# A gated recurrence of 512 steps: the first groups' input products put in front of half A's and half B's first products

## The chip, the cores and the metric

The kernel runs on one core of one Trainium2 chip. The metric is the device time of one execution in microseconds (us), the median over several runs. A lower number is better.

## The reference

A recurrence over 512 time steps for 8 sequences, with 512 input values and 512 state values each; its output is added to the input.

```python
def step(h, x_t):
    fused = sigmoid(concat([x_t, h]) @ w_W + w_b)
    hidden_state, output_state = split(fused, 2)          # r and z below
    memory_state = x_t @ wx_W + wx_b + hidden_state * (h @ wh_W + wh_b)
    h_new = output_state * h + (1.0 - output_state) * tanh(memory_state)
    return (h_new, h_new)

out = x + scan(step, cond, x)      # x: (8, 512, 512), cond: (8, 512), all float32
```

Each step needs three products with the state h (for r, z and the memory term) and three with the input x_t. Only those with h hang on the step before.

## The kernel before, in words

**Halves and banks.** The 512 state values are split into half A and half B. The state of each half is in the tiles `hTA` and `hTB`, one for each of eight steps in turn. The products with the state go to three PSUM banks: A (192 columns: memory term, z and r of half A; weights `wa`), B (128 columns: r and the memory term of half B) and C (64 columns: z of half B; in the tile `cs`). The weights of B and C are in `wb`. A product such as A0 or B2 names the bank and the quarter k of the state that it multiplies; k = 0 and 1 are in `hTA`, 2 and 3 in `hTB`. Each is four matmuls (`mm`, line 217) on four column tiles of TensorE, and the trace has two records for a matmul. The function `mm` issues all matmuls, so all have line 217 and are told apart by their tiles.

**Order in a step.** TensorE takes the products of a step in the order `ORDER`, and then some work on the inputs of later steps. The first step has an order of its own, `FIRST`, in which `x` stands for one part of input products. The schedule is manual: every engine does its instructions in the order in which the program lists them, and the framework adds the waits.

**Gates.** For each half, VectorE transposes r, the memory term and z out of PSUM (`turn_r`, `turn_h`, `turn_z`; lines 407 and 423), ScalarE takes the sigmoids, VectorE scans r times the memory term (`memory`), ScalarE takes the tanh, and a second scan (`update`, both line 391) makes the new state, on which the next step's products wait. Half B's gates come behind half A's on VectorE, and `update` of half A behind half B's `turn_r` and `turn_h`. GpSimd adds x (line 545) and SyncE stores.

**Input products.** Four steps make a group. Group g's products with `wx` are accumulated in `xps[g % 2]` (tiles `xp`), a PSUM tile with 384 columns of products (`XC`) that is first filled with the bias: `seed(g)`, a ScalarE copy. Groups 0 to 3 are plain products: `prefill(g)` is a generator of four parts (k = 0 to 3), each four matmuls of 384 columns, and `take(it, n)` issues n parts. From group 4 on the products of two groups are made together from seven products of sums (`x_step`, `product`), which need sums of weights: `weight_sum(n)` on VectorE, into the tiles `tw`, and sums of inputs on GpSimd. A finished group is copied by ScalarE to `even` or `odd`, from there into the banks A, B and C of the group's steps (`spread`), and VectorE transposes its memory term out of it (`turn_x`, line 280). Group 0 is read straight from `xps[0]`, and in the first step the A products are accumulated in `xps[0]` itself (`to`, `pa`).

**The start.** `warm()` is a product with zeros. SyncE's queue brings `wx` in four parts, `wa` in four parts, `wb` in two and the second half of chunk 0's inputs (`load_x(0, 1)`, which holds groups 2 and 3), in this order; the first half comes with the initial state in `head`, by ScalarE's queue. Chunks 1 to 3 follow in the first steps. Group 1's parts stand between the A products of the first step and behind it; groups 2 and 3 stand behind steps 1 to 4, two parts a step.

```python
        if i < 5:
            take(first[(i + 3) // 2], 2)
        if i > 3:
            x_step(*divmod(i, 2 * GS))
```

Of the kernel before, what the change touches and what calls it, by code (L numbers as in the profile page):

```python
# [24 lines left out]

ORDER = "A0 B0 A1 A2 A3 B1 B2 B3 C0 C1 C2 C3"

FIRST = "A0 x A1 x A2 x A3 B0 B1 B2 B3 C0 C1 C2 C3"

BANKS = {"A": 192, "B": 128, "C": 64}  # L30

# [3 lines left out]
XC = slice(64, 448)  # L35
# [14 lines left out]
XP = {"A": slice(0, 192), "X": slice(192, 320), "C": slice(320, 384), "B": slice(384, 512)}  # L50
# [3 lines left out]
def tile_cond_rnn_residual(  # L54
# [39 lines left out]
    nc = tc.nc  # L94
# [30 lines left out]
    def load_x(c, half=slice(0, 2)):  # L125

        if c < NCH:
            if c not in xins:
                xins[c] = xin_p.tile([P, 2, NQ, TC * B // 2], F32, tag="xin", name=f"xin_{c}")
            nc.sync.dma_start(  # L130
                out=xins[c][:, half], in_=x[c].rearrange("p (e k n) -> p e k n", e=2, k=NQ)[:, half]
            )

    def x_of(c, k, t, n):

        e, t = divmod(t, TC // 2)
        if c == 0 and e == 0:
            first = head[:, :NX].rearrange("p (k n) -> p k n", k=NQ)
            return first[:, k, t * B : (t + n) * B]
        return xins[c][:, e, k, t * B : (t + n) * B]  # L140
# [10 lines left out]
    wa = const.tile([P, NQ, NQ, 192], F32, name="wa")  # L151
    for k in range(NQ):
        nc.sync.dma_start(out=wa[:, k], in_=wa_d[k])
    wb = const.tile([P, NQ, NQ, 192], F32, name="wb")
    nc.sync.dma_start(out=wb[:, :3], in_=wb_d)
    nc.sync.dma_start(out=wb[:, 3], in_=wb3_d)

    def wh(bank, k, j):
        return wa[:, k, j] if bank == "A" else wb[:, k, j, {"C": slice(0, 64), "B": slice(64, 192)}[bank]]

    load_x(0, 1)

    def pair(n, name, rows, slots):

# [32 lines left out]
    even = const.tile([P, 512], F32, name="even")  # L197
    odd = const.tile([P, 512], F32, name="odd")

    def state(hf, i, slot=2):  # L200

        s = i % GS
        return hT[hf][i % NH][:, B * s : B * s + B, :, slot]
# [9 lines left out]
    xps = [psum.tile([P, 512], F32, name=f"xp{q}") for q in range(2)]  # L213
    eps = psum.tile([P, 512], F32, name="eps")[HI, :W]

    def mm(out_, lhsT, rhs, start=False):
        nc.tensor.matmul(  # L217
            out_, lhsT, rhs, start=start, stop=False, skip_group_check=True
        )
# [4 lines left out]
    def warm():  # L224

        mm(xps[1], zeros[:, :128], zeros)
# [18 lines left out]
    def act(key, out_, in_, func, **kw):  # L245
        inst = nc.scalar.activation(out_, in_, func, **kw).ins  # L246
        if key in written:
            tc.declare_no_dep(inst, written[key], reason="ordered through VectorE")
        written[key] = inst
        return inst  # L250

    def seed(g):

        nc.scalar.copy(xps[g % 2], bias)  # L254

    def prefill(g):

        c, t0 = divmod(g * GS, TC)
        for k in range(NQ):
            for j in range(NQ):  # L260
                mm(
                    xps[g % 2][32 * j : 32 * j + 32, XC],
                    x_of(c, k, t0, GS),
                    wx[:, k, j, :],
                )
            yield

    def source(g):

        return xps[0] if g == 0 else (even, odd)[g % 2]  # L270

    def spread(g, names):

        for n in names:
            nc.scalar.copy(banks[g % 2][n], source(g)[:, XP[n]])

    def turn_x(g, hf):

        c0 = XP["X"].start + HU * hf
        nc.vector.transpose(  # L280
            md1[hf][g % 2][:, :, :, 1].rearrange("p n c -> p c n"), source(g)[:, c0 : c0 + HU]
        )
# [4 lines left out]
    def wx_of(kh, ch):  # L287
        return wx[:, 2 * kh : 2 * kh + 2, 2 * ch : 2 * ch + 2]
# [5 lines left out]
    def weight_sum(n, k=slice(0, 2), j=slice(0, 2)):  # L294

        a, b = [
            (wx_of(0, 1), wx_of(0, 0)),
            (wx_of(1, 1), tw[0]),
            (wx_of(1, 1), wx_of(0, 1)),
            (wx_of(1, 0), tw[1]),  # L300
        ][n]
        nc.vector.tensor_tensor(tw[n][:, k, j], a[:, k, j], b[:, k, j], ALU.subtract)
# [44 lines left out]
    def take(it, n=None):  # L347
        while n is None or n > 0:
            if next(it, it) is it:
                return  # L350
            n = None if n is None else n - 1

    seed(1)
    take(prefill(0))
    warm()
    first = {g: prefill(g) for g in (1, 2, 3)}
    weight_sum(2)
    weight_sum(0)
    spread(0, "BCA")
    for hf in range(2):  # L360
        turn_x(0, hf)

    pool_done = {}
    for i in range(T):
        g, s = divmod(i, GS)
        c, t = divmod(i, TC)
        ps = banks[g % 2]
# [4 lines left out]

        for n in (ORDER if i else FIRST).split():
            if n == "x":
                take(first[1], 1)
                continue
            bank, k = n[0], int(n[1])
            hs = hT[k // 2][i % NH][:, :, k % 2, 2]
            for j in range(NQ):
                to = ps[bank] if i or bank != "A" else xps[0][:, XP["A"]]  # L380
                mm(to[32 * j : 32 * j + 32, :], hs, wh(bank, k, j))
        if i < 5:
            take(first[(i + 3) // 2], 2)
        if i > 3:
            x_step(*divmod(i, 2 * GS))

# [2 lines left out]
        def scan(c_, out_, d0, d1):  # L389

            return nc.vector.tensor_tensor_scan(  # L391
                *[t_[:, :, c_].rearrange("p n c s -> p (n c s)") for t_ in (out_, d0, d1)],
                0.0,
                ALU.mult,
                ALU.add,
            ).ins

        pa = ps["A"] if i else xps[0][:, XP["A"]]
        raw = {
            "h": (pa[:, :HU], ps["B"][:, HU:]),  # L400
            "z": (pa[:, HU : 2 * HU], ps["C"]),
# [3 lines left out]
        def turned(n, hf):  # L405
            t_ = work.tile([P, 2, 32], F32, tag=f"t{n}{hf}", name=f"t{n}{hf}_{i}")
            inst = nc.vector.transpose(t_.rearrange("p c n -> p (c n)"), raw[n][hf]).ins  # L407
            return t_[:, :, rows], inst
# [4 lines left out]
        def turn_r(hf):  # L413
            tr, _ = turned("r", hf)
            r_done[hf] = act(
                ("r", hf, g % 2, s),
                md0[hf][g % 2][:, rows, :, 1].rearrange("p n c -> p c n"),
                tr,
                AF.Sigmoid,
            )  # L420
# [27 lines left out]
        def memory(hf, q):  # L448

            c_ = slice(q, q + 1)  # L450
            scan(c_, ms[hf], md0[hf][g % 2][:, rows], md1[hf][g % 2][:, rows])
            act(("n", hf, q, i % NH), state(hf, i, 1)[:, :, c_], ms[hf][:, :, c_, 1], AF.Tanh)
# [8 lines left out]
        turn_z(0)  # L461
        memory(0, 0)
        memory(0, 1)
        turn_r(1)
        turn_h(1)
        update(0, 0)
        turn_z(1)
        tc.add_manual_dep(update(0, 1), r_done[1].name, SYNC)
        if i == 0:

            seed(2)
        if i == T - 1:
            nc.gpsimd.tensor_tensor(
                ot[:, t, :2, :].rearrange("p c n -> p n c"),
# [13 lines left out]
        o, u = divmod(i, 2 * GS)  # L488
        nxt, two = o + 1 < NG // 2, o + 2 < NG // 2
        if i == 0:  # L490
            nc.scalar.copy(odd[:, XC], xps[1][:, XC])
        if u == 0:
            spread(2 * o + 1, "AC")
            turn_x(2 * o + 1, 0)
            turn_x(2 * o + 1, 1)
        elif u == 1:
            if o and nxt:
                nc.vector.tensor_tensor(reg(GA), reg(BE), more[HI], ALU.add)
                nc.scalar.copy(even[LO, XC], reg(AL))
            spread(2 * o + 1, "B")  # L500
        elif u == 2:
            if o == 0:
                nc.scalar.copy(even[:, XC], xps[0][:, XC])
                seed(3)
            elif nxt:
                nc.vector.tensor_tensor(odd[HI, XC], reg(GA), both[LO], ALU.add)
                nc.scalar.copy(both[HI], reg(DE))
            if two:
                x_sum(o + 2, 2)
        elif u == 3:  # L510
            if two:
                nc.scalar.copy(reg(AL), bias[LO, XC])
                x_sum(o + 2, 0)
        elif u == 4:
            if o == 0:
                nc.scalar.copy(odd[:, XC], xps[1][:, XC])
            elif nxt:
                nc.vector.tensor_tensor(even[HI, XC], reg(BE), both[HI], ALU.add)
            if two:
                nc.scalar.copy(reg(DE), step_bias[HI])  # L520
        elif u == 5 and nxt:
            if o:
                nc.scalar.copy(odd[LO, XC], reg(GA))
            spread(2 * o + 2, "A")
            turn_x(2 * o + 2, 0)
        elif u == 6 and nxt:
            spread(2 * o + 2, "BC")
            turn_x(2 * o + 2, 1)
            if two:
                nc.scalar.copy(more[HI], eps)  # L530
                x_sum(o + 2, 1)
        elif u == 7 and nxt:
            if two:
                nc.scalar.copy(reg(BE), reg(AL))
                nc.scalar.copy(both[LO], reg(DE))
                x_sum(o + 2, 3)
# [105 lines left out]
```

## Time and profile before

| | us |
|---|---|
| median of 3 runs (lowest, highest) | 1657.39 (1656.86, 1657.92) |
| the profiled execution: its own time | 1659.38 |
| its span in the trace | 1657.4 |
| TensorE matmuls busy | 1645.1 (99% of the span) |
| TensorE weight loads busy (beside the matmuls) | 1487.9 (90%) |
| ScalarE busy | 1198.4 (72%) |
| VectorE busy | 1152.0 (70%) |
| GpSimd busy | 303.2 (18%) |

The engines are PE (TensorE matmuls), PEld (TensorE weight loads), DVE (VectorE), ACT (ScalarE), POOL (GpSimd) and SP (SyncE, which issues DMAs). Rows of a timeline give start and duration in us, the engine, the line of the kernel, the operation, output<-input with the program's tile names, shapes and the count of records merged; in brackets stands the idle time before it and what ended it. Rows of windows give the stretch, its length, the busy time and count of PE, PEld, DVE, ACT and POOL, the granted TensorE clock as a share of full speed, the DMA share and GB/s. Times of several records merged count from the first start to the last end, so a pipelined group's duration is longer than the time by which it holds up the next.

### The profile page before, as it was taken

To read this page: it belongs to the slowest core of one execution; us is meant where nothing else is said; L and a number is where in the kernel's file an instruction comes from. 1 tells how busy PE (TensorE), PEld (TensorE's weight loads), DVE (VectorE), ACT (ScalarE), POOL (GpSimd) and SP (SyncE) were. 2 spreads that over 40 slices of the span, in tenths; PEclk is the share of its full clock that TensorE was granted. 3 is DMA by queue.
4 is the path that set the end of the run, shared out by engine and by line. 5 is a ranking of instruction groups with operands and counts; after the bars stand their busy time and mean duration, and the time that the engine had idled before them with its cause. 6 is when DMAs were issued, how large, how long until landed. Compare 5 with 4: busy or idle time off the path is not lost.

```text
span 1657.4 us, 126070 instructions
## 1 busy us (share of the span) xinstructions
PE 1645.1 (99%) x54253; PEld 1487.9 (90%) x54253; DVE 1152.0 (70%) x9193; ACT 1198.4 (72%) x6009; POOL 303.2 (18%) x1283
## 2 busy tenths in 40 slices
PE   8999999999999999999999999999999999999998
PEld 5999999999888889999999999999999999989987
DVE  5776676676766766767667667676676676766766
ACT  4777777777777777777777777777777777777775
POOL 1211111111111111111111111111111111111111
PEclk9999999999999999999999999999999999999999
DMA  4000000000000000000000000000000000000000
GB/s 182 11 14 17 15 14 15 17 15 14 14 16 16 14 14 16 16 14 14 16 16 14 15 16 16 15 14 16 16 15 14 16 16 15 14 16 11 10 10 10
DMA packets 37287, 31.16 MB, mean 19 GB/s; under 512 B 4084, under 2 KB 35060, under 8 KB 36600
## 3 DMA queue, kind: packets, MB, share of 16 engines
q1 hardware_dynamic: 36576, 22.95, 4.5%
q8 instruction: 424, 6.95, 1.7%
q14 instruction: 135, 1.11, 0.2%
q10 hardware_dynamic: 152, 0.16, 0.0%
HBM read 14.70 MB, written 8.39 MB: 14 GB/s over the span
## 4 chain that ended last, share of the span: by engine, by line
PE 98%; DVE 1%; DMA 1%; issue 0%; ACT 0%; SPq 0%
PE A L217 40%; PE B L217 26%; PE xp L217 17%; PE cs L217 13%; PE eps L217 1%; DMA wx<-in_wx_dram 1%; DVE tr L407 0%; DVE m L391 0%; DVE tz L407 0%; DVE md1B L423 0%; DVE hTA L391 0%; DVE md1A L423 0%; SPq L149 0%; ACT hTB L246 0%; ACT xp L254 0%
## 5 line engine op out<-in xcount | busy, mean ns | idle before, releaser
L217 PE MATMUL A<-wa,hTA 128*32 128x192 f32 x8176 | 547.6, 326 | 2.1 <-DVE hTA L391 2.1
L217 PE MATMUL A<-wa,hTB 128*32 128x192 f32 x8176 | 440.7, 326 | 0.0
L217 PE MATMUL B<-wb,hTA 128*32 128x128 f32 x8192 | 440.6, 273 | 0.0
L217 PEld LDWEIGHTS A<-wa,hTA 128*32 128x32 f32 x8176 | 281.3, 122 | 129.8 <-DVE hTA L391 103.7
L407 DVE STREAM_TRANSPOSE tr<-A 128x64 f32<-128x64 f32 x511 | 127.6, 250 | 369.4 <-PE A L217 369.4
L545 POOL TENSOR_TENSOR ot<-xin,hTB 128x16 f32<-128x16 f32 x503 | 125.9, 250 | 1309.3 <-DVE hTB L391 989.0
L217 PEld LDWEIGHTS B<-wb,hTA 128*32 128x32 f32 x8192 | 337.5, 122 | 5.7
L217 PEld LDWEIGHTS A<-wa,hTB 128*32 128x32 f32 x8176 | 323.0, 122 | 13.0 <-DVE hTB L391 0.4
L217 PE MATMUL B<-wb,hTB 128*32 128x128 f32 x8192 | 332.2, 273 | 0.0
L217 PE MATMUL xp<-tw,sx 128*32 128x96 f32 x1488 | 267.5, 433 | 0.0
L217 PEld LDWEIGHTS B<-wb,hTB 128*32 128x32 f32 x8192 | 255.1, 122 | 0.0
L246 ACT ACTIVATE md0A<-tr 128x16 f32<-128x16 f32 x512 | 112.3, 219 | 191.3 <-DVE tr L407 177.4
L391 DVE TENSOR_TENSOR_SCAN hTB<-hd0B,hTB 128x24 f32<-128x24 f32 x1024 | 157.8, 195 | 100.5 <-ACT hTB L246 100.5
L217 PE MATMUL cs<-wb,hTA 128*32 128x64 f32 x8192 | 222.9, 219 | 0.0
L217 PE MATMUL cs<-wb,hTB 128*32 128x64 f32 x8192 | 222.8, 219 | 0.0
L217 PE MATMUL xp<-wx,xin 128*32 128x384 f32 (+2 forms) x1304 | 219.6, 425 | 0.0
L217 PEld LDWEIGHTS cs<-wb,hTA 128*32 128x32 f32 x8192 | 200.4, 122 | 0.0
L391 DVE TENSOR_TENSOR_SCAN hTA<-hd0A,hTA 128x24 f32<-128x24 f32 x1024 | 190.1, 186 | 0.0
L246 ACT ACTIVATE hd0B<-tz 128x16 f32<-128x16 f32 x512 | 116.0, 227 | 93.3 <-DVE tz L407 93.3
L246 ACT ACTIVATE hTB<-hTB 128x16 f32<-128x16 f32 x512 | 120.1, 234 | 78.9 <-DVE hTB L391 53.1
L217 PEld LDWEIGHTS cs<-wb,hTB 128*32 128x32 f32 x8192 | 173.0, 122 | 0.0
L246 ACT ACTIVATE hTA<-m 128x8 f32<-128x8 f32 x1024 | 160.6, 206 | 2.8 <-DVE m L391 0.5
(105 smaller groups left out, 2664.3 us busy)
## 6 DMA issues: line engine op xcount, KB each, us to landing
out_dram<-ot SPq DMA_DIRECT2D x128, 64.0 KB, 1.6
xin<-in_x_dram SPq DMA_DIRECT2D x112, 64.0 KB, 2.2
wx<-in_wx_dram SPq DMA_DIRECT2D x4, 768.0 KB, 6.9
wa<-in_wa_dram SPq DMA_DIRECT2D x4, 384.0 KB, 8.9
wb<-in_wb_dram SPq DMA_DIRECT2D x1, 1152.0 KB
xin<-in_x_dram SPq DMA_DIRECT2D x3, 256.0 KB, 8.3
wb<-in_wb_dram SPq DMA_DIRECT2D x1, 384.0 KB, 11.2
head<-in_xh_dram ACTq DMA_DIRECT2D x1, 144.0 KB, 4.9
```

The source lines that it names most:

```text
L217: nc.tensor.matmul(out_, lhsT, rhs, start=start, stop=False, skip_group_check=True)
L246: inst = nc.scalar.activation(out_, in_, func, **kw).ins
L391: return nc.vector.tensor_tensor_scan(*[t_[:, :, c_].rearrange("p n c s -> p (n c s)") for t_ in (out_, d0, d1)], 0.0, ALU.mult, ALU.add,).ins
L407: inst = nc.vector.transpose(t_.rearrange("p c n -> p (c n)"), raw[n][hf]).ins
L545: return engine.tensor_tensor(ot[:, t, 2 * hf : 2 * hf + 2, :].rearrange("p c n -> p n c"), x_of(c, slice(2 * hf, 2 * hf + 2), t, 1).rearr ...
```

## The change

Group 1's four parts are issued whole behind group 0's, before the first step, and `warm()` is dropped. The first step's order becomes all of A, then group 2's four parts, then B and C. Group 3's parts come one a step behind steps 1 to 4, and the first step has no part behind C. The first step's A products go to bank A, like those of all steps. The second half of chunk 0 is loaded before `wb`. On VectorE the first weight sum follows the two `turn_x` and the second stands in the first step between the halves' gates. On ScalarE `seed(2)`, the copy of group 1 to `odd` and `seed(3)` come before the first step; group 2's copy to `even` takes the place that group 1's copy had behind the first step. From step 5 on every engine has the same instructions in the same order as before.

```diff
-FIRST = "A0 x A1 x A2 x A3 B0 B1 B2 B3 C0 C1 C2 C3"
+FIRST = "A0 A1 A2 A3 x x x x B0 B1 B2 B3 C0 C1 C2 C3"
...
         nc.sync.dma_start(out=wa[:, k], in_=wa_d[k])
+    load_x(0, 1)
     wb = const.tile([P, NQ, NQ, 192], F32, name="wb")
     nc.sync.dma_start(out=wb[:, :3], in_=wb_d)
     nc.sync.dma_start(out=wb[:, 3], in_=wb3_d)
...
-    load_x(0, 1)
...
     seed(1)
     take(prefill(0))
-    warm()
-    first = {g: prefill(g) for g in (1, 2, 3)}
-    weight_sum(2)
-    weight_sum(0)
-    spread(0, "BCA")
+    take(prefill(1))
+    first = {g: prefill(g) for g in (2, 3)}
+    spread(0, "ABC")
     for hf in range(2):
         turn_x(0, hf)
+    weight_sum(2)
+    seed(2)
+    nc.scalar.copy(odd[:, XC], xps[1][:, XC])
+    seed(3)
...
             if n == "x":
-                take(first[1], 1)
+                take(first[2], 1)
                 continue
...
-                to = ps[bank] if i or bank != "A" else xps[0][:, XP["A"]]
-                mm(to[32 * j : 32 * j + 32, :], hs, wh(bank, k, j))
-        if i < 5:
-            take(first[(i + 3) // 2], 2)
+                mm(ps[bank][32 * j : 32 * j + 32, :], hs, wh(bank, k, j))
+        if 1 <= i < 5:
+            take(first[3], 1)
...
-        pa = ps["A"] if i else xps[0][:, XP["A"]]
+        pa = ps["A"]
...
         memory(0, 1)
+        if i == 0:
+            weight_sum(0)
         turn_r(1)
...
-        if i == 0:
-
-            seed(2)
...
         if i == 0:
-            nc.scalar.copy(odd[:, XC], xps[1][:, XC])
+            nc.scalar.copy(even[:, XC], xps[0][:, XC])
...
         elif u == 2:
-            if o == 0:
-                nc.scalar.copy(even[:, XC], xps[0][:, XC])
-                seed(3)
-            elif nxt:
+            if o and nxt:
```

## The prediction

> **What bounds the kernel now.** I read the profile's page first, then the chain of waits in order of time, then the timeline of the first 40 us, then the windows with the granted clock, and last the DMA issues.
>
> ```profile
> span 1657.4 us, 126070 instructions
> PE 98%; DVE 1%; DMA 1%; issue 0%; ACT 0%; SPq 0%
> ```
>
> The chain that ended last is TensorE (PE) for 98% of the span, so outside the first microseconds the time is the sum of PE's instructions. One step in order of time, first steps, then a later one:
>
> ```profile
> 23.07 0.88 PE A L217 x16
> 23.94 0.65 PE B L217 x24
> ...
> 30.25 0.33 PE A L217 x8
> 30.57 0.22 PE B L217 x8
> 30.79 0.97 PE A L217 x24
> 31.76 0.65 PE B L217 x24
> 32.42 0.45 PE cs L217 x32
> 32.87 1.29 PE xp L217 x16
> 34.16 0.33 PE A L217 x8
> ...
> 44.60 0.33 PE A L217 x8
> ...
> 47.22 0.65 PE xp L217 x7
> 47.87 0.33 PE A L217 x8
> ```
>
> Columns: start, duration, engine, tile, records (a matmul leaves two). The step that starts at 30.25 lasts 3.91 us without a hole: 2.62 for A, B and C (cs), then 1.29 for two parts of plain x products. The step at 44.60 carries 0.65 of x work and lasts 3.27. So a part of plain x products (4 matmuls, 8 records) is 0.65 us, a whole group of four parts 2.58, the A products of a step 1.31 (0.33 + 0.97), B 0.87, C 0.45, and a step is as long as PE's work in it.
>
> PE is not full only at the start. The timeline there:
>
> ```profile
> 11.15 0.85 PE L217 MATMUL xp<-wx,head 128*32 128x384 f32 x8 [0.48 <-DMA wx<-in_wx_dram]
> 11.23 3.43 DVE L302 TENSOR_TENSOR tw<-wx 128x1536 f32<-128x1536 f32 x2 [2.01 <-DMA wx<-in_wx_dram]
> 12.34 0.33 ACT L275 COPY A<-xp 128x192 f32<-128x192 f32 x1
> 14.74 0.21 DVE L280 STREAM_TRANSPOSE md1B<-xp 128x64 f32<-128x64 f32 x1
> 15.05 0.86 PE L217 MATMUL xp<-wa,hTA 128*32 128x192 f32 x8 [1.99 <-issue]
> 19.99 0.64 PE L217 MATMUL B<-wb,hTA 128*32 128x128 f32 x16
> 20.25 0.25 DVE L407 STREAM_TRANSPOSE tr<-xp 128x64 f32<-128x64 f32 x1 [5.30 <-PE xp L217]
> 21.12 0.25 DVE L407 STREAM_TRANSPOSE tr<-B 128x64 f32<-128x64 f32 x1
> 21.64 0.14 PEld L217 LDWEIGHTS A<-wa,hTA 128*32 128x32 f32 x4 [0.19 <-DVE hTA L391]
> 21.98 0.59 ACT L254 COPY xp<-bias 128x512 f32<-128x512 f32 x1
> 22.81 0.31 DVE L391 TENSOR_TENSOR_SCAN hTB<-hd0B,hTB 128x24 f32<-128x24 f32 x2 [0.73 <-ACT hTB L246]
> 23.07 0.51 PEld L217 LDWEIGHTS A<-wa,hTB 128*32 128x32 f32 x16 [0.41 <-DVE hTB L391]
> ...
> 23.28 0.46 ACT L491 COPY odd<-xp 128x384 f32<-128x384 f32 x1
> ...
> 24.81 0.23 DVE L407 STREAM_TRANSPOSE tr<-B 128x64 f32<-128x64 f32 x1
> 25.89 0.31 DVE L391 TENSOR_TENSOR_SCAN hTB<-hd0B,hTB 128x24 f32<-128x24 f32 x2 [0.20 <-ACT hTB L246]
> ```
>
> Three losses show. First, group 0's products end about 11.8 (11.15 + 0.65). A0 starts only at 15.05, just after VectorE's transposes out of xp end at 14.95 (14.74 + 0.21): the two weight sums, 3.43 us, stand ahead of them. Second, from 15.05 to 19.99 PE does A's 32 records and three parts of x, which at the prices above are 1.31 + 1.94 = 3.25, in 4.94: 1.69 lost. The windows say why; the third column from the right is the granted clock:
>
> ```profile
> 13.00:15.00 2.00, 0.06 (x1) 0.00 (x0) 1.95 (x3) 0.00 (x0) 0.00 (x0) 1.00 1.11 455
> 15.00:16.00 1.00, 0.95 (x12) 0.72 (x16) 0.00 (x0) 0.00 (x0) 0.00 (x0) 0.56 1.00 424
> 16.00:17.00 1.00, 1.00 (x12) 0.32 (x8) 0.00 (x0) 0.00 (x0) 0.00 (x0) 0.50 0.93 393
> 18.00:19.00 1.00, 1.00 (x16) 0.55 (x12) 0.00 (x0) 0.00 (x0) 0.00 (x0) 0.73 1.06 398
> ```
>
> After two idle microseconds the clock is 0.50 from about 15.1 (0.56 is 12% of a microsecond at full and the rest at half) to about 18.5 (0.73 is 54% at half). Third, step 1's A products with half B's state wait until 23.07. Between the transpose of B and the scan that makes this state lie 1.69 us in step 0 (21.12 to 22.81), 1.08 in step 1 (24.81 to 25.89). The difference, 0.61, is the seed copy of 0.59 that ScalarE runs at 21.98 ahead of the tanh.
>
> **The change, part by part.** *Weight sums behind the transposes, and A into its own bank.* The A products now write bank A, so they wait for ScalarE's copy of A (0.33, right after 11.8, so done before 12.7 even where it was last) and no longer for the transposes. What hides the sum that stays ahead of step 0 (1.72, half of 3.43): step 0's first transpose, not due before about 15.9. The other half sits on VectorE between half A's gates and half B's; before, 0.8 us pass from the transpose at 20.25 to the end of those gates, so it runs about 16.8 to 18.5, and B's transpose is due at 19.4: free, and if that cover were gone at most 1.72.
>
> *Group 1's products whole before A.* The 2.58 fill the hole from 11.80 to 14.38. The removed filler product was in that hole and costs nothing. Group 1's inputs and wx are there already; ScalarE seeded its accumulator before group 0. Then A's four products, 1.31, provided wa has landed:
>
> ```profile
> 3.03 3.46 SPq L153 DMA_DIRECT2D wa<-in_wa_dram  x4
> 6.54 0.43 SPq L155 DMA_DIRECT2D wb<-in_wb_dram  x1
> 7.37 0.33 SPq L156 DMA_DIRECT2D wb<-in_wb_dram  x1
> 9.27 4.03 SPq L130 DMA_DIRECT2D xin<-in_x_dram  x4
> ...
> wa<-in_wa_dram SPq DMA_DIRECT2D x4, 384.0 KB, 8.9
> ...
> wb<-in_wb_dram SPq DMA_DIRECT2D x1, 384.0 KB, 11.2
> ```
>
> The last wa issue ends at 6.49; with 8.9 to land it is there at about 15.0, the first at about 11.9. A3 is due at 15.36, so A ends at 15.69. PE has no hole in this stretch, so I take the clock at full and the 1.69 as won.
>
> *Group 2's products before B, and x's second half of chunk 0 ahead of wb on SyncE's queue.* It is 128 KB; at the 398 to 424 GB/s of the windows it takes a third of a microsecond, so it lands some 0.3 behind wa, near 15.3, before it is due at 15.69. What is moved past it is wb: both issues come one place later (7.37 and 9.27 instead of 6.54 and 7.37; the queue of transfers is still full then) and land 0.3 later. The last 384 KB of wb landed at 18.57 (7.37 + 11.2), now about 18.9. Seed 2, 0.59, moved from step 0 to ScalarE's start, follows the transposes, so it is done by about 14. The x block runs 15.69 to 18.27, then B 18.27 to 19.14; B's fourth product is due at 18.27 + 3 x 0.22 = 18.93, even with wb. C ends at 19.59. The copy of group 1 and seed 3, ScalarE's other moved instructions (0.46 and 0.59), can start when group 1's products end at 14.38 and end about 15.6, before the first sigmoid at 16.2; the copy of group 2 takes the place that group 1's had. GpSimd's and the later SyncE orders stay.
>
> *Into step 1.* Before, the first weight load of step 1 came 1.65 after B's start (21.64 to 19.99): now 19.92, so 0.33 of idling after C, since step 0 has no x part behind C. A0, B0, A1 take 0.33 + 0.22 + 0.33 and end at 20.80. Half B's state: B's transpose 1.13 after B's start, 1.08 to the scan with the seed gone, 0.26 to PE (22.81 to 23.07): 18.27 + 2.47 = 20.74. So those A products start at 20.80 instead of 23.07: 2.27 won.
>
> *Steps 1 to 4.* Each loses one of its two x parts: 4 x 0.65 = 2.58. They become 3.27, the length of the step at 44.60. Their waits fit: half B's state would be needed about 2.0 after B's end (C 0.45, x 0.65, then 0.88) and takes about 1.6.
>
> Sum: 2.27 + 2.58 = 4.85. The bound from below in time is PE without any hole (another 0.33, and up to 0.23 where step 1's block of 0.88 returns to 0.65): a gain of 5.4. The bound above: wb or x half a microsecond later, 4.3. The profiled execution took 1659.38 with a span of 1657.4; the median of the runs without a profile is 1657.39. I take the 4.85 from that median: 1652.5.
>
> [...] The 0.50 clock followed a hole of 1.99 us. [...]
>
> **Rivals.** *The slow clock is no gain.* Either it comes back in the same place, or the executions without a profile lose less to it than the profiled one. For it: the fall at 15.1 and the rise at 18.5 need not fall so in each run, and the unprofiled runs are 2 us shorter than the profiled one. Against it: they lie within 1.06 of each other. Price 1.69: 1654.2. Chance 0.14.
>
> *Steps 1 to 4 do not shrink*, because with less x work behind C the chain through VectorE and ScalarE becomes the bound. For it: the weight sums of these steps add VectorE work. Against it: the step at 44.60 is step 7, which carries such a sum too, and it lasts 3.27. Only 2.27 is left: 1655.1. Chance 0.06.
>
> *Slower: the x block waits for its transfer.* Group 2's products stand ahead of B on PE's strict order, so B, C and step 1 queue behind the landing of x's second half. Each microsecond past 15.69 costs one; the gain is gone if it lands at 20.5, and at about 18.9 if the hole also halves the clock (another 1.69); slower by 0.2% from about 22. Had it landed at the old place it would be 9.27 + 9.7:
>
> ```profile
> xin<-in_x_dram SPq DMA_DIRECT2D x1, 128.0 KB, 9.7
> ```
>
> That is 18.97, and with the slow clock 1657.5; at 22.3 it would be 1660.8. Against it: the issue comes ahead of 1536 KB of wb. [...] Chance 0.04 for an end slower than before by over 0.2%, and 0.04 for a milder form within 0.2%.
>
> **How the numbers follow.** The forecast has 0.72. From 1657.39, 0.2% is 3.3 us, about what a measurement of this kernel tells from no change, so faster means under 1654.1. The forecast's own range is 1651.5 (gain 5.4, half a microsecond of scatter) to 1653.6. To hold 8 in 10 the range reaches to the first rival, 1654.5. Faster: 0.72 and 0.06 of the first rival's 0.14, whose 1654.2 lies on the bound, so 0.78; same: its other 0.08, the second rival's 0.06 and the milder 0.04, so 0.18; slower: 0.04.
>
> **What would show it.** In the profile after: no hole on PE between 11.15 and about 18; clock 1.00 in all windows from 11 to 20; A starting near 14.4, the x block at 15.7, B at 18.3; step 1's second A half at 20.8; steps 2 to 5 starting 3.27 apart; from step 5 on all as before but 4.9 earlier. Wrong would be a hole ahead of the x block or of B, a clock of 0.50, steps 1 to 4 above 3.4, or a later step of another length.

## The result, and the profile after

| | before | after |
|---|---|---|
| median of 21 runs each, on one chip (us) | 1657.92 (1656.83 to 1660.06) | 1656.12 (1655.05 to 1657.49) |
| ratio after / before, 95% interval | | 0.9987 (0.9981 to 0.9993) |
| profiled execution, own time / span | 1659.38 / 1657.4 | 1655.30 / 1653.5 |

The change wins 1.80 us, about 0.1%, where 4.9 were forecast. The time lies above the range. The sign was right; by the prediction's bound of 0.2% the outcome is "same".

The page of the kernel after has the same bound as before:

```profile
span 1653.5 us, 126068 instructions
...
q8 instruction: 424, 6.95, 1.7%
...
PE 98%; DMA 1%; DVE 1%; issue 0%; ACT 0%; SPq 0%
```

The chain is still PE. The 1% of DMA in it was there before too, but then it was the load of `wx` and now it is that of `wb`. The row of `q8` gives a queue's packets, megabytes and share of 16 DMA engines; the prediction passed it by. The timeline of the kernel after shows where the DMA comes in:

```profile
11.11 3.43 PE L217 MATMUL xp<-wx,head 128*32 128x384 f32 x40 [0.39 <-DMA wx<-in_wx_dram]
...
14.36 0.83 PE L217 MATMUL A<-wa,hTA 128*32 128x192 f32 x16
...
15.66 2.76 PE L217 MATMUL xp<-wx,xin 128*32 128x384 f32 x32
...
16.63 1.74 DVE L302 TENSOR_TENSOR tw<-wx 128x1536 f32<-128x1536 f32 x1
...
19.49 0.66 PE L217 MATMUL B<-wb,hTA 128*32 128x128 f32 x16 [1.07 <-DMA wb<-in_wb_dram]
...
20.27 0.19 PEld L217 LDWEIGHTS B<-wb,hTB 128*32 128x32 f32 x8 [0.16 <-DMA wb<-in_wb_dram]
...
20.78 0.25 DVE L408 STREAM_TRANSPOSE tr<-B 128x64 f32<-128x64 f32 x1 [2.41 <-PE B L217]
...
22.00 0.31 DVE L392 TENSOR_TENSOR_SCAN hTB<-hd0B,hTB 128x24 f32<-128x24 f32 x2 [0.26 <-ACT hTB L246]
...
22.26 0.51 PEld L217 LDWEIGHTS A<-wa,hTB 128*32 128x32 f32 x16 [0.23 <-DVE hTB L392]
```

Group 1's products fill the hole, A starts at 14.36 and the x block at 15.66, within 0.03 of the forecast. Then B, due at 18.27, starts at 19.49: it waits for `wb`. Step 1's second A half starts at 22.26 instead of 20.80. The windows of the kernel after, with the columns of before, say that the clock is not the reason:

```profile
15.00:16.00 1.00, 1.00 (x31) 0.70 (x23) 0.09 (x1) 0.73 (x2) 0.00 (x0) 1.00 1.02 433
...
18.00:19.00 1.00, 0.42 (x8) 0.00 (x0) 0.37 (x1) 0.00 (x0) 0.00 (x0) 1.00 1.01 379
```

It is 1.00 in both (0.56 and 0.73 before), PE is idle from 18.42, and the DMA share is 1.01: the engines still have loads to bring. The chain of waits of the kernel after, in order of time (start, duration, what):

```profile
7.42 12.02 DMA wb<-in_wb_dram
19.49 1.27 PE B L217 x32
...
24.88 0.33 PE A L217 x8
...
27.50 0.65 PE xp L217 x8
28.14 0.33 PE A L217 x8
...
31.41 0.33 PE A L217 x8
...
34.67 0.15 PE A L217 x2
```

Steps 2, 3 and 4 last 3.26, 3.27 and 3.26, as forecast. Step 5 starts at 34.67; the forecast's place was 38.06 (before) less 4.85, so 33.21, and the difference, 1.46, is that of the second A half. From step 5 to the end it is 1618.8 (1653.5 less 34.67), against 1619.3 before.

### The profile page after: what moved, and what is told of

The parts are those of the page before. It is cut to its first block, busy times and chain, and to the rows that moved or that the text cites. A ratio compares the mean times of both kernels' runs of the same rounds, so it can differ in the third digit from the quotient of the medians.

```text
span 1653.5 us, 126068 instructions
## 1 busy us (share of the span) xinstructions
PE 1642.8 (99%) x54251; PEld 1476.2 (89%) x54251; DVE 1153.8 (70%) x9193; ACT 1199.0 (73%) x6009; POOL 302.8 (18%) x1283
## 3 DMA queue, kind: packets, MB, share of 16 engines
q8 instruction: 424, 6.95, 1.7%
## 4 chain that ended last, share of the span: by engine, by line
PE 98%; DMA 1%; DVE 1%; issue 0%; ACT 0%; SPq 0%
PE A L217 40%; PE B L217 27%; PE xp L217 17%; PE cs L217 13%; DMA wb<-in_wb_dram 1%; PE eps L217 1%; DMA wx<-in_wx_dram 0%; DVE tr L408 0%; DVE m L392 0%; DVE md1B L424 0%; DVE hTA L392 0%; DVE tz L408 0%; DVE md1A L424 0%; ACT hTB L246 0%; SPq L149 0%
## 5 line engine op out<-in xcount | busy, mean ns | idle before, releaser
L217 PE MATMUL B<-wb,hTA 128*32 128x128 f32 x8192 | 434.5, 273 | 1.1 <-DMA wb<-in_wb_dram 1.1
L217 PEld LDWEIGHTS A<-wa,hTA 128*32 128x32 f32 x8192 | 276.1, 122 | 132.2 <-DVE hTA L392 106.6
L217 PEld LDWEIGHTS B<-wb,hTA 128*32 128x32 f32 x8192 | 330.2, 122 | 11.0 <-DMA wb<-in_wb_dram 1.8
L217 PEld LDWEIGHTS A<-wa,hTB 128*32 128x32 f32 x8192 | 318.1, 122 | 16.7 <-DVE hTB L392 0.2
```

Source lines behind the costliest of these rows:

```text
L217: nc.tensor.matmul(out_, lhsT, rhs, start=start, stop=False, skip_group_check=True)
```

## What was tried

Two questions were open: why `wb` landed 1.2 to 1.4 later than forecast, and why the medians differ by 1.80 where the two traces differ by 3.39 at step 5 (38.06 less 34.67).

For the first there were two theories. A: PE fetches its own instructions by DMA, in packets of 16 KB (6.95 MB / 424, the row of `q8`); 54,251 matmuls and as many weight loads are 256 instructions a packet (and a kernel below with 112 more of them has 425 packets). The change has PE work through its instructions earlier, so that the first fetch falls into the last microseconds of `wb`'s load. B: the load moved ahead of `wb` costs more than its bytes. The DMA views (queue, packets, megabytes, share of 16 engines) show the fetch; the first two lines are of the kernel after, 17 to 18.4 us:

```profile
q1 hardware_dynamic: 182, 0.48, 86.9%
q8 instruction: 1, 0.02, 3.9%
```

The kernel before, in the same stretch, and then from 20 to 21.4:

```profile
q1 hardware_dynamic: 295, 0.54, 99.0%
...
q8 instruction: 1, 0.02, 4.7%
```

One packet took 3.9% of 16 engines over 1.4 us, 0.87 us of one engine. The 182 load packets took 0.11 us each (86.9% of 22.4, by 182), so the fetch holds its engine for the time of eight of them. Before, this fetch came at 20.16, after `wb`. The end of the loads shows an engine that is behind. These are the GB/s in forty slices of 0.1 us from 20 to 24, of the kernel before and of the kernel after:

```profile
GB/s 328 410 246 123 21 0 0 0 0 0 0 0 0 0 0 0 0 0 0 0 0 0 0 0 0 0 0 0 0 0 0 0 0 0 0 0 0 0 0 82
```
```profile
GB/s 266 205 205 103 41 21 41 20 20 20 21 41 20 20 20 41 0 0 0 0 0 0 0 164 0 0 0 0 0 0 0 82 0 0 0 0 0 0 0 0
```

Before, the loads end together by 20.5. After, from there to 21.7, some 20 GB/s are left, which is one packet of 2 KB in a slice: from 20.5 to 21.7 the load queue's 17 packets took 6.4% of 16 engines, 1.02 of one, so by this estimate a single engine still has them to bring when the others are done. (The 164 and the 82 are later fetches.)

For the second question: theory 1, all executions of the kernel before have the slow clock of its profile; theory 2, only a part has it, and the others start B earlier than 19.99, so that the change finds less to win.

### The kernel before once more

> The kernel before, unchanged, profiled a second time. Theory 1 (the slow clock after the 2 us hole belongs to the hole): again granted clock 0.50 from about 15 to 18.5, B starting near 20.0, span near 1657.4. [...]

Measured: 1659.2, span 1657.3. Its windows and chain:

```profile
16.00:17.00 1.00, 1.00 (x20) 0.65 (x16) 0.00 (x0) 0.00 (x0) 0.00 (x0) 1.00 0.94 396
```
```profile
18.58 0.91 PE B L217 x32
...
21.46 0.88 PE A L217 x16
...
36.76 0.15 PE A L217 x2
```

In the profile that the forecast was made from, the same view has

```profile
20.19 0.91 PE B L217 x32
```

The clock is 1.00 after the same hole of 1.99. B and the second A half start 1.61 earlier (18.58 against 20.19, 21.46 against 23.07) and step 5 starts 1.30 earlier; of the 0.31 between, the profile shows only that a weight load of step 1 stood 0.25 for no reason that it gives. Theory 2 holds as far as one execution can show it. Against this execution the change wins 2.09 at step 5 (36.76 less 34.67).

### Only the load moved

```diff
         nc.sync.dma_start(out=wa[:, k], in_=wa_d[k])
+    load_x(0, 1)
     wb = const.tile([P, NQ, NQ, 192], F32, name="wb")
...
-    load_x(0, 1)
```

> The kernel before with one part of the change alone: the second half of chunk 0 loaded ahead of wb. Theory A (PE's instruction fetch, a 16 KB packet on one of the 16 DMA engines, is what made wb late): the last part of wb lands 0.3 to 0.4 us later than before's 18.57, near 18.9, since the fetch still comes at about 20.2. Theory B (the later issue of wb, 7.4 and 9.3 instead of 6.5 and 7.4, made it late): it lands near 20.3, some 11 us after its issue. Time as before in both, 1657 to 1658, as B is not due before 20.

Measured: 1659.65, span 1657.8. The DMA issues, with KB and the time from issue to landing, and SyncE's timeline:

```profile
wb<-in_wb_dram SPq DMA_DIRECT2D x1, 384.0 KB, 9.7
```
```profile
9.13 0.33 SPq L157 DMA_DIRECT2D wb<-in_wb_dram  x1
```

The last part lands at 18.83 (9.13 + 9.7), 0.26 after the 18.57 of before: the 0.3 of the forecast. The fetch is at 19.97 here. Theory B falls. This execution had the slow clock:

```profile
16.00:17.00 1.00, 1.00 (x16) 0.60 (x12) 0.00 (x0) 0.00 (x0) 0.00 (x0) 0.50 1.04 442
```

### The fetch moved, the load left in place

Twenty-eight small zero products are added to the kernel before, 14 in each of two places in the start where PE waits anyway.

```diff
+    def pad(n):
+        for q in range(n):
+            r = slice(32 * (q % 4), 32 * (q % 4) + 32)
+            mm(xps[1][r, :16], zeros[:, :32], zeros[:, :16])
...
     warm()
+    pad(14)
     mm(xps[0], ones.rearrange("p j m -> p (j m)"), rows4, start=True)
+    pad(14)
```

> The kernel before with 28 small products of zeros in the first 8 us, 112 more PE instructions, DMAs as before. They bring PE's first instruction fetch from 20.2 to about 17.4, into the transfer of wb. Theory A: the last part of wb lands 1.0 to 1.5 us later than before's 18.57, at 19.6 to 20.1, with the issue unchanged at 7.4. Theory B: it stays at 18.6. Time within 0.5 us of before in both.

Measured: 1659.39, span 1657.5. The fetch came at 13.42, earlier than intended but also inside the loads. The DMA issue and the chain:

```profile
wb<-in_wb_dram SPq DMA_DIRECT2D x1, 384.0 KB, 12.0
```
```profile
7.76 12.00 DMA wb<-in_wb_dram
19.80 0.48 PE B L217 x8
...
22.26 0.87 PE A L217 x16
```

With SyncE's order untouched, `wb`'s last part now lands at 19.76 (18.57 before; 18.66 and 19.4 in the two further profiles of the kernel before, the later one with `wx` itself 0.75 late). Not all of that is the fetch: the issue of this part came at 7.76 instead of 7.37, because the loads ahead of it were late. From issue to landing it took 12.0, against 11.2 in all three profiles of the kernel before, so the fetch costs 0.8. B's last products wait for `wb`, and the second A half starts at 22.26, 0.80 later than in the first further profile, 0.3 of it from the later issue. So here a fetch inside the loads delayed `wb`, by 0.8, without any load being moved.

### The load moved, the fetch held back

The kernel after, with the products of groups 1 and 2 behind the first step, and three zero products in each of their old places, so that PE stays busy with fewer instructions. ScalarE's copy of group 1 and `seed(3)` move behind the first step with them.

```diff
-FIRST = "A0 A1 A2 A3 x x x x B0 B1 B2 B3 C0 C1 C2 C3"
+FIRST = "A0 A1 A2 A3 w w w B0 B1 B2 B3 C0 C1 C2 C3 x x x x x x x x"
...
-    take(prefill(1))
-    first = {g: prefill(g) for g in (2, 3)}
+    for _ in range(3):
+        warm()
+    first = {g: prefill(g) for g in (1, 2, 3)}
```

> The changed kernel with groups 1 and 2's products behind the first step's C, and three products of zeros in each of their places: PE is as busy until B, but has done some 104 fewer instructions, so that its first instruction fetch comes after wb. Theory A: fetch at 19 or later, wb at 17.8 to 18.0 and its last part at 18.8 to 19.0, B done by 19.3 instead of 20.4. Rival (wb is late in this order of loads for another reason): wb's last part at 20.2 as before. The time is 2 to 4 us above the changed kernel in both, since 5.2 us of products stand behind C then.

Measured: 1663.09, span 1661.2, longer because the x work is not done in the holes. The DMA issues and SyncE's timeline:

```profile
wb<-in_wb_dram SPq DMA_DIRECT2D x1, 1152.0 KB, 10.6
wb<-in_wb_dram SPq DMA_DIRECT2D x1, 384.0 KB, 9.7
```
```profile
7.43 0.33 SPq L156 DMA_DIRECT2D wb<-in_wb_dram  x1
9.28 0.33 SPq L157 DMA_DIRECT2D wb<-in_wb_dram  x1
```

The issues are where the kernel after has them (7.42 and 9.27), the fetch is at 20.03, and the two parts land at 18.03 and 18.98. In the kernel after they landed at 19.42 and 20.27 (12.0 and 11.0 from issue). So the forecast's landing of 18.9 was right for the move of the load alone, and the last part is 1.3 later where the fetch comes early.

### The fillers alone, and the weight sums alone

The first has two more zero products in the hole of the kernel before; the second moves only the weight sums, as the change does.

```diff
-    warm()
+    for _ in range(3):
+        warm()
```

> The kernel before with two more products of zeros behind the one that stands after group 0's products (a microsecond and a half more of PE work in the hole of 2 us before A0, nothing else). If the slow clock came from that hole: granted clock 1.00 in every window from 11 to 20, B starting near 18.6 instead of 20.0 in the slow-clock executions. Theory 1 (the slow clock is in nearly every execution of before): 1.6 us under before. Theory 2 (in about half of them: 2 of 4 profiles so far show it): 0.5 to 1.0 under before.

```diff
-    weight_sum(2)
-    weight_sum(0)
     spread(0, "BCA")
     for hf in range(2):
         turn_x(0, hf)
+    weight_sum(2)
...
         memory(0, 1)
+        if i == 0:
+            weight_sum(0)
         turn_r(1)
```

> The kernel before with one part of the change alone: on VectorE the transposes ahead of the weight sums, the second sum in the first step. The hole before A0 closes (A0 near 12.7 instead of 15.0). Without a collision B could start when wb lands, near 17.6, and the time would fall by 0.8 against executions of before without the slow clock and 2.4 against those with it. Theory A (PE's instruction fetch comes by PE's progress, and so moves from 20.2 to about 17.8, into the last part of wb): the last part of wb lands near 19.5 instead of 18.6, B's last product waits for it, and only the slow clock's share is left, 0.3 to 1.2 under before.

Measured, against the 1662.49 of the kernel before beside them: with the fillers 1661.09, ratio 0.9992 (0.9983 to 1.0000); with the sums moved 1660.90, ratio 0.9987 (0.9978 to 0.9996). The windows and the chain with the fillers, then the chain with the sums:

```profile
15.00:16.00 1.00, 1.00 (x20) 0.68 (x24) 0.00 (x0) 0.00 (x0) 0.00 (x0) 1.00 1.02 433
```
```profile
18.41 0.87 PE B L217 x32
...
21.28 0.87 PE A L217 x16
...
36.27 0.15 PE A L217 x2
```
```profile
8.01 11.20 DMA wb<-in_wb_dram
19.25 0.48 PE B L217 x8
...
21.70 0.87 PE A L217 x16
```

With the hole filled without useful work the clock stayed at 1.00 and B started at 18.41, as in an execution of the kernel before that kept its clock (18.58). Bringing A forward by moving the sums won nothing at the second A half (21.70 against 21.46): B waits for `wb` there too. But that wait is not the fetch's, as had been expected: the fetch came at 18.54, and `wb`'s last part, issued at 8.01 because `wx` was some 0.6 late, landed 11.2 after its issue, as in the kernel before. So a fetch 0.7 ahead of the landing delayed nothing that shows here.

How often the hole costs the clock shows in the mean granted clock of each execution, since 3.4 us at half (15.1 to 18.5 in the profile of the forecast) cost 0.001 of the span. It was 0.999 or less in 37 of 65 executions of the kernel before, and in 8 of 56 of the kernels whose hole is filled (the three zero products, the kernel after twice, and the two variants below), so a few executions have this mean for another reason. In the three sets of runs the executions of before with the lower clock took 1.60, 0.81 and 0.86 longer in the mean. The 21 executions of before in the result have no clock on record.

### The kernel after again

> The changed kernel, unchanged, profiled and timed again. Theory A: the first instruction fetch comes again near 17.4, wb lands near 19.4 and B starts near 19.5 instead of 18.3; span 1653.5 to 1654.5. If wb lands near 17.9 this time, its lateness was chance. Time 1655.5 to 1656.5, 1.5 to 2.5 us under before.

Measured: 1658.54 against 1660.40, ratio 0.9985 (0.9976 to 0.9994), and on another chip, beside the variants, 1659.11 against 1661.83, ratio 0.9990 (0.9982 to 0.9998). In their profiles the fetch is at 17.72 and 17.95, the last part of `wb` lands at 20.2 and 20.05, and step 5 starts at 34.65 and 34.49: the late last part of `wb` is there each time, 10.9 and 10.5 after its issue instead of 9.7. The first part landed 10.6 after its issue in both, as with a late fetch, so that B started in time (18.32 and 18.59) and only its last product waited. That the first part was late as well (12.0) is particular to the profile of the result.

> The changed kernel once more, as the reference on this chip for the next two. First instruction fetch near 17.5, last part of wb at 20.2, step 5 starting at 34.7; 1.5 to 2.5 us under before.

### Filling the wait for wb with more x work

If `wb` cannot come before 19.4, two parts of group 3 fit ahead of B. The rest of group 3 is then two parts for four steps, half a part each. One variant halves a part by column tiles (two of four), the other by columns (192 of 384 on all four column tiles).

```diff
-FIRST = "A0 A1 A2 A3 x x x x B0 B1 B2 B3 C0 C1 C2 C3"
+FIRST = "A0 A1 A2 A3 x x x x y y B0 B1 B2 B3 C0 C1 C2 C3"
...
-            yield
+                if j % 2:
+                    yield
```

> The changed kernel with two of group 3's four parts also put before B, into the wait for wb, and the other two spread as halves of a part over steps 1 to 4. Theory A (the end of the first step is set by the landing of wb's last part, 20.2, whatever PE does until then): PE is busy through until 19.5, step 1's second A half starts at 22.2 to 22.4 as in the changed kernel, steps 1 to 4 are 2.95 instead of 3.27: 1.3 us under the changed kernel, 3.0 to 3.4 under before. Rival (the steps are then bound by VectorE and ScalarE): steps of 3.2, no gain over the changed kernel.

```diff
+            w = W // 2 if g == 3 and k > 1 else W
+            for c0 in range(0, W, w):
+                for j in range(NQ):
...
+                        wx[:, k, j, c0 : c0 + w],
+                    )
+                yield
```

> The changed kernel with two of group 3's four parts before B, and the other two parts cut into halves by columns (192 of 384, on all four column tiles) over steps 1 to 4; halves by column tiles had cost 0.65 like whole parts. Theory A (the first step's end is set by wb's landing, so PE work put ahead of B is free): step 1's second A half at 22.2 to 22.4, steps 1 to 4 of 2.95 to 3.0 instead of 3.27, step 5 starting at 33.4 to 33.7 instead of 34.7: 1.0 to 1.3 us under the changed kernel. Rival (without 0.65 of x a step is bound by VectorE and ScalarE at 3.2): step 5 at 34.4 or later, no gain.

Measured: by column tiles 1659.43 against 1662.49, ratio 0.9986 (0.9977 to 0.9995); by columns 1658.31 against 1661.83, ratio 0.9981 (0.9972 to 0.9990). The chain by column tiles, then by columns:

```profile
19.89 1.04 PE B L217 x32
...
24.41 0.62 PE xp L217 x3
...
34.80 0.17 PE A L217 x3
```
```profile
24.18 0.33 PE xp L217 x8
...
29.84 0.59 DVE m L394 x2
30.43 0.14 DVE tr L410
30.57 0.13 DVE md1B L426
30.70 0.18 DVE hTA L394
...
30.93 0.55 PE A L217 x8
```

Half a part on two column tiles takes 0.62, a whole part on four 0.65 (the row at 27.50 of the kernel after), so that variant wins nothing: step 5 starts at 34.80. Half the columns take half the time, 0.33. There steps 2 to 4 would be 2.94, but they last 3.08, 3.35 and 3.33: VectorE's and ScalarE's chain for the state of half A is now late, as in the second rival of the prediction, one part further down. Step 5 starts at 34.26, 0.2 before the kernel after on that chip. Of all kernels this one has the lowest ratio to before; its interval overlaps that of the kernel after (0.9990), so that it is better is not shown.

## Why the prediction was right and wrong

**Right: the hole, the clock, steps 2 to 4.** Group 1's products, A at 14.38, the x block at 15.69, ScalarE's and VectorE's moved instructions beside them, and 3.27 a step came as worked out. The first and third rival did not come in their plain forms: the clock was 1.00, and the x block did not wait. The hole of 1.99 was followed by a clock of 0.50 in two of the five profiles that have it (the three of the kernel before, and those with the load or the fetch moved alone) and by 1.00 in the other three, and with the hole filled the clock was 1.00 in all profiles. What decides in which executions it falls, no run shows.

**Wrong: "What is moved past it is wb ... land 0.3 later".** The move of the load cost 0.26 (18.83), as said. What the step left out is that the kernel's own instructions come by DMA beside the loads (3.9% of 16 engines from 17 to 18.4, the loads 86.9%), and that the fetch moved forward with PE's work (20.16 to 17.38). What it cost in the end is the last part of `wb`: it landed at 20.27 instead of 18.9, B's last product waited for it, and the second A half started at 22.26 instead of 20.80. That is the 1.46 at step 5: 4.85 becomes 3.39. That B's start was 1.22 late too changed nothing: where B started in time (18.32), step 5 came no earlier (34.65). The prediction did say that a hole ahead of B would prove it wrong, and gave "`wb` or x half a microsecond later" as its bound; that bound was too near: it had no term for what else uses the engines.

**Wrong: "I take the 4.85 from that median".** The sum was made against a profiled execution with the slow clock, 1.46 above the median of the compared runs, and 1.69 of it is the slow clock's. An execution of before without it starts step 5 1.30 earlier and leaves 2.09 to win. With the lower clock in 37 of 65 executions, 3.39 and 2.09 mix to an estimate of 2.8. This is the first rival's second form, which had 0.14 and shared its price. The profiled time standing 2 us above the median of the runs fitted it but does not show it: a later profile of the kernel before stands 1.85 above its median (1664.34, 1662.49) and has no slow clock. The first loss came on top, so the time lies beyond the rival's 1654.2.

**What is left over.** 2.8 would be expected, and 1.80, 1.86 and 2.72 were measured; 2.8 lies inside all three intervals (the first reaches to 3.1). Of the miss of 3.62 (1656.12 less 1652.5), 0.53 is that the kernel before was itself at 1657.92 in the compared runs, 1.46 is `wb`, about 0.6 the mix of clocks (4.85 less 1.46 less 2.8), and 1.0 is not accounted for. Two things bear on that 1.0, and neither is settled. If the 21 executions of before in the result, whose clock is not on record, had all kept it, no more than 2.09 was there to win, near the 1.80. And 2.09 may be high: the kernel with the fillers, which also kept its clock, starts step 5 at 36.27, which would leave 1.60.

## What to carry to other kernels

In these runs the load that filled the DMA engines (share 1.01) shared them with the instruction fetch, which moved when work on PE was moved (20.16 to 17.38): work brought forward while weights are still landing can delay those weights, here by 0.8 to 1.3. Before a sum is taken off a median, see whether the profiled execution has the median's events: profile the kernel more than once, since one profile had a slow clock that another of the same kernel lacked, and the time alone did not tell them apart (1659.38 with it, 1659.20 and 1664.34 without). And filling a hole is worth at most the distance to what lands next: here the clock was 1.00 with the fill, and the wait moved to the following weights (1.07 ahead of B).

## What the runs showed of the hardware

**The fetch.** Counted in the traces, PE had started 202 to 350 matmuls and weight loads at its first fetch (266 in the kernel after, 222 in its profile before), and 1974 to 2021 at its eighth (2002 after, 2008 before), near eight times the 256 of the packet counts, in the thirteen profiles of these kernels. The place of the first is looser, and why is open: the first further profile of the kernel before had its fetch at 20.31 with 350 started, the profile of the forecast at 20.16 with 222, so the count alone does not set it. That the fetch moves when PE's instructions are moved is shown (13.42 to 20.56); by what rule is not. No delay of `wb` shows where the fetch came after `wb` had landed or 0.7 before (11.2 from issue to landing, 9.7 with the load moved); where it came earlier the last part of `wb` took 0.8 to 1.3 longer from issue to landing (12.0 against 11.2 with no load moved; 10.5 to 11.0 against 9.7 with the load moved).

**Column tiles.** Half a part on two of four column tiles held PE for 0.62, a whole part on four for 0.65. Halving the columns instead halved the time, to 0.33.

**Open.** From step 5 on the instruction streams are the same, yet single profiled executions, on several chips, took 1618.8 (after), 1619.3 (before), 1620.5 (before again), 1622.3 and 1622.7 (after again) and 1625.2 (before, a third time) from there to the end. In the last of them PE's weight loads have short waits that the profile puts down to nothing it shows (20 from 60 to 1650, 4.6 in all; in the profile of the forecast one of 0.2, after the change none), and no run tells why the times differ. The last of these executions is this one:

> The kernel before, unchanged, profiled a third time, to count the slow clock: theory 1: clock 0.50 from about 15; theory 2: either. With the slow clock B starts near 20.0 and the mean granted clock of the execution rounds to 0.999, without it near 18.6 and 1.000.

Measured: 1664.34, span 1662.4, no slow clock, step 5 at 37.19. That scatter is larger than what the change won, so starts of steps in the traces were compared here, and times only over many runs.
